# Half-column products in one turn, slice means before W_v W_out, and row factors in all partitions: a change to a graph-attention and slice-attention kernel on one core

## The chip, the core and the metric

One core of a Trainium2 chip runs the whole program. The metric is the device time in microseconds. Every comparison below is made between runs that interleave with the kernel before on the same chip; all runs quoted are in the fast state. The kernel before takes some 2726 us; its runs lie between 2719 and 2735 us, and the sessions' medians between 2724.5 and 2729.7. So I compare ratios within a session where a few us matter.

## The reference

A batch is 512 rows of 256 features; there are 32 batches, each computed alone:

```python
x = x + gnn(layernorm(x), adj, ...)      # two attention layers with residuals
x = x + ffn(layernorm(x), ...)           # slice attention
# gnn: relu(x W1) -> attention without mask (h = x W_fc, e = leaky_relu(f1_i + f2_j))
#      -> elu(elu()) + residual -> relu(. W2) -> attention with mask adj -> residual
# ffn: w = softmax over 64 slices, for 8 heads; tokens = weighted means of fx over rows
#      q, k, v = token W_q, W_k, W_v; att = softmax(q k / 8); out_slice = att v
#      result = (out_slice spread back by w) W_out + b_out
```

All data are float32.

## The kernel before

The kernel does not issue its instructions in program order. It records every operation of all batches with a name of its step ("xnT", "pT" and so on are tiles; "h2", "e", "tokens" are steps), gives each a priority from a table of turns plus the number of its batch times a period, and lets a list scheduler with costs of its own choose, once, at build time, the order on each engine. Each engine then runs its fixed list, waiting on semaphores only. Instructions of three or four batches are thus mixed on every engine. Two more tuples, HEAD and TAIL, shift the priorities of the first and last batches.

```python
TURNS = {"load": -182.4, ..., "h2": -4.8, "e": 4.9, ..., "out": 181.5}
PERIOD, SPARE = 88.0, 0.00
HEAD, TAIL = (-3.1, -0.9, -0.1), (-1.0, -1.3, -1.0)
...
KEPT = 1
...
def start_of(op):                       # in the scheduler
    t = op.ready
    for log in op.logs:                 # the tiles that op uses
        if log not in until:            # not yet allocated
            kept = self.KEPT if log.bufs > self.KEPT and op.age > oldest and log.psum else 0
            if len(slots[log.tag]) <= kept or turn[log.queue][0] is not log:
                return None             # cannot start
```

`op.age` is the batch and `oldest` the oldest unfinished one. So **a batch that is not the oldest may never take the last free PSUM tile of a kind**. There are three kinds, and the rule holds for those with more than one tile:

```python
def mm_tile(shape): return psum.tile(shape, F32, tag="mm", name="mm", bufs=5)
def tr_tile(shape): return psum.tile(shape, F32, tag="tr", name="tr", bufs=2)
def sm_tile(shape): return psum.tile(shape, F32, tag="sm", name="sm", bufs=1)
```

The parts that the change touches are the row factors of the first attention, the logits f2b of the second, the slice tokens with half-column products, and the end of slice attention (shortened):

```python
# factors: exp of 4 numbers a row; two of them are then spread to all partitions
nc.scalar.activation(ex, ex, AF.Exp)
for s in range(2):
    pt = tr_tile([P, N])
    for i in range(NT):
        nc.tensor.transpose(pt[:, ts(i)], ex[:, s, i:i+1].to_broadcast([P, P]), ident)
    nc.scalar.copy(acb[:, s, :], pt)

# h2: logits of the second attention
f2b = new("f2b", [P, N])                                   # SBUF
pt = tr_tile([P, N])
for j in range(NT):
    nc.tensor.transpose(pt[:, ts(j)], h[:, j, D+1:D+2].to_broadcast([P, P]), ident)
nc.scalar.copy(f2b, pt)
# e: for each of four row tiles
nc.vector.scalar_tensor_tensor(e, f2b, h[:, i, D:D+1], mbias[:, i, :], ...)
...
if by_dma("e", b):                      # transposed by DVE blocks and a round trip in DRAM
    flip(e, stage[:, :, ts(i, Q)]); continue
pt = tr_tile([P, NT, P])                # only in the first and the last batch (EDGES):
for j in range(NT):                     # transposed on PE
    nc.tensor.transpose(pt[:, j, :], e[:, ts(j)], ident)

# tokens: 16 products of 64 columns (half of PE's columns) a batch
nc.tensor.matmul(pm[ts(s, C), p, :]..., wfx[:, k, ts(2*p+s, C)], s1T[:, k, :]..., ...)
# vo, gg: tokens times W_v W_out (256 wide), then attention times that (256 wide)
nc.tensor.matmul(pv[:, s, :], tokbd[:, p, :], wvo[:, p, :], start=True, stop=True)
...
nc.tensor.matmul(pg[:, s, :], attT[:, p, :], vo[:, p, :], start=True, stop=True)
```

## Time and profile before

| | before |
|---|---|
| time, median of 3 | 2728.61 us (2726.51 to 2730.74) |
| PE in use | 98% of the span |
| period of a batch in the steady part | 83.1 us |
| all waits of PE | 52 us, of them 13 in 20 steady batches |

The prediction below shows the lines. One thing to know for reading them: a record of PE has a modelled end that overlaps the next record, so neither durations nor their sum tell what an instruction takes from the stream. The distance from start to start does. From those distances I take a nominal pitch for each kind (0.217 us a record of 256 or 257 columns, and so on). The rest of PE's time, labelled waits and unlabelled excess over the pitch together, I call **lost**. This split is used after the result.

### The profile page before, as it was taken

What the parts mean: (1) busy time and instruction counts of PE and PEld (TensorE: products, weight loads), DVE (VectorE), ACT (ScalarE), POOL (GpSimd) and SP (SyncE); (2) the same over time, 40 slices, a digit from 0 to 9 for tenths busy, and PEclk for the clock granted to TensorE, in tenths of its full rate; (3) what the DMA queues carried; (4) which work ended last, traced back from release to release, by engine and by line L of the source; (5) the groups of instructions that cost most, each with busy time, mean ns of one, the idle gap of its engine ahead of it and who ended that gap; (6) DMA issues with size and microseconds to landing.
All of it is one profiled execution on the core that took longest, in us unless ns stands there. A gap on an engine that the chain in (4) does not pass through costs nothing.

```text
span 2725.3 us, 34426 instructions
## 1 busy us (share of the span) xinstructions
PE 2667.5 (98%) x11965; PEld 1988.7 (73%) x11965; DVE 2057.3 (75%) x5126; ACT 1117.4 (41%) x2102; POOL 124.6 (5%) x233
## 2 busy tenths in 40 slices
PE   7999999999999999999999999999999999999997
PEld 5777777777777777777777777777777777777765
DVE  6577777887777877778877778777788777787775
ACT  3443344443444443444434444334444334444332
POOL 1000000000000000000000000000000000000000
PEclk9999999999999999999999999999999999999998
DMA  5226555645555555556454555555565555564521
GB/s 167 58 57 165 135 140 143 168 133 154 139 148 139 148 154 139 138 145 165 133 153 130 158 139 145 157 140 141 147 161 134 158 137 145 140 156 137 133 78 53
DMA packets 465077, 375.35 MB, mean 138 GB/s; under 512 B 86532, under 2 KB 382088, under 8 KB 464904
## 3 DMA queue, kind: packets, MB, share of 16 engines
q1 hardware_dynamic: 461568, 371.01, 51.2%
q10 hardware_dynamic: 3336, 2.14, 0.3%
q8 instruction: 95, 1.56, 0.2%
q14 instruction: 78, 0.64, 0.1%
HBM read 197.96 MB, written 175.11 MB: 137 GB/s over the span
## 4 chain that ended last, share of the span: by engine, by line
PE 73%; DMA 13%; DVE 9%; SPq 2%; issue 2%; ACT 1%; ACTq 0%; POOL 0%; DVEq 0%; POOLq 0%
PE mm L255 70%; DMA o1T<-scr 4%; DMA scr<-s_stage 3%; SPq L255 2%; PE tr L255 2%; DMA s1T<-scr 2%; DVE u L255 1%; DMA w_raw<-scr 1%; DVE u_stage L255 1%; DVE xn L255 1%; DMA scr<-u_stage 1%; DVE xn_stage L255 1%; PE sm L255 1%; DVE vo L255 1%; DVE o1T L255 0%
## 5 line engine op out<-in xcount | busy, mean ns | idle before, releaser
L255 PE MATMUL mm<-wfc,o0T 128*128 128x257 f32 x2048 | 486.1, 379 | 0.0
L255 PEld LDWEIGHTS mm<-wfc,o0T 128*128 128x128 f32 x2048 | 386.2, 189 | 131.1 <-issue 84.9
L255 PE MATMUL mm<-h,pT 128*128 128x257 f32 (+1 forms) x2048 | 467.3, 382 | 0.4 <-ACT u L255 0.2
L255 PEld LDWEIGHTS mm<-h,pT 128*128 128x128 f32 x2048 | 379.9, 189 | 63.1 <-ACT u L255 4.8
L255 DVE TENSOR_TENSOR x<-mm,x 128x512 f32<-128x512 f32 x64 | 44.2, 691 | 292.8 <-PE mm L255 292.8
L255 PE MATMUL mm<-xnT,w 128*128 128x512 f32 x512 | 249.3, 602 | 2.1 <-ACT xnT L255 1.8
L255 PE MATMUL mm<-weff,xn2T 128*128 128x512 f32 x512 | 251.3, 594 | 0.0
L255 PE MATMUL mm<-xn,w 128*128 128x257 f32 x1024 | 244.7, 382 | 4.8 <-DVE w L255 4.8
L255 PE MATMUL mm<-h,p2T 128*128 128x257 f32 x1024 | 242.0, 380 | 0.7 <-ACT p2T L255 0.7
L255 ACT COPY h<-mm 128x257 f32<-128x257 f32 (+1 forms) x384 | 142.2, 370 | 241.2 <-PE mm L255 237.2
L255 PE MATMUL mm<-o1T,w 128*128 128x512 f32 x512 | 227.8, 597 | 10.1 <-DVE o1T L255 9.9
L255 PE MATMUL mm<-gg,wT 128*128 128x256 f32 x1024 | 235.9, 379 | 0.0
L255 PEld LDWEIGHTS mm<-xn,w 128*128 128x128 f32 x1024 | 191.4, 190 | 36.4 <-ACT w L255 5.7
L255 PEld LDWEIGHTS mm<-gg,wT 128*128 128x128 f32 x1024 | 189.6, 190 | 35.1 <-issue 6.5
L255 PEld LDWEIGHTS mm<-h,p2T 128*128 128x128 f32 x1024 | 187.0, 190 | 28.2 <-ACT p2T L255 0.9
L255 PEld LDWEIGHTS mm<-o1T,w 128*128 128x128 f32 x512 | 94.9, 190 | 126.3 <-issue 91.1
L255 DVE STREAM_TRANSPOSE o_stage<-o2T 128x512 f32<-128x512 f32 x64 | 45.6, 712 | 171.0 <-ACT o2T L255 171.0
L255 ACT ACTIVATE e<-e,nmax 128x512 f32<-128x512 f32 x128 | 92.5, 723 | 199.6 <-DVE nmax L255 199.4
L255 ACT ACTIVATE m<-m 128x512 f32<-128x512 f32 x192 | 120.3, 627 | 131.0 <-DVE m L255 130.9
L255 PEld LDWEIGHTS mm<-xnT,w 128*128 128x128 f32 x512 | 92.6, 191 | 68.8 <-issue 50.9
L255 ACT ACTIVATE m<-m,neg 128x512 f32<-128x512 f32 x192 | 138.0, 719 | 3.6
L255 DVE SCALAR_TENSOR_TENSOR u<-m,u 128x512 f32<-128x512 f32 x192 | 131.6, 686 | 9.1 <-ACT m L255 7.7
(144 smaller groups left out, 3917.7 us busy)
## 6 DMA issues: line engine op xcount, KB each, us to landing
scr<-xn_stage SPq DMA_DIRECT2D x240, 128.0 KB, 2.7
scr<-u_stage SPq DMA_DIRECT2D x120, 256.0 KB, 4.3
o1T<-scr SPq DMA_DIRECT2D x30, 1024.0 KB, 6.0
scr<-e_stage SPq DMA_DIRECT2D x120, 256.0 KB, 4.2
p2T<-scr SPq DMA_DIRECT2D x30, 1024.0 KB, 5.4
scr<-w_stage SPq DMA_DIRECT2D x120, 256.0 KB, 4.2
w_raw<-scr SPq DMA_DIRECT2D x30, 1024.0 KB, 6.7
xt<-in_x_dram SPq DMA_DIRECT2D x32, 512.0 KB, 4.6
```

The costliest lines, as they stand in the source:

```text
L255: getattr(getattr(self.nc, op.engine), op.method)(*op.args, **op.kwargs)
```

## The change

The intent: take instructions out of PE's stream, which is the bound. The half-column products are given one priority so that they come in one turn; half as many transposes spread the row factors, by exponentials in all partitions; attention is applied to the 64-wide tokens before they are multiplied by W_v W_out. Two side effects matter later. SBUF is full, so the new tile meanbd takes the room of f2b, which now **stays in the PSUM tile of its transposes**. And turns, period and shifts were chosen anew. The diff is shortened, and some of its lines are put in words:

```diff
-    "load": -182.4, "norm1": -141.0, ... "h2": -4.8, "e": 4.9, ... "out": 181.5,
+    "load": -225.4, "norm1": -221.3, ... "h2": -55.6, "e": -48.0, ... "out": 160.2,
-PERIOD, SPARE = 88.0, 0.00
-HEAD, TAIL = (-3.1, -0.9, -0.1), (-1.0, -1.3, -1.0)
+PERIOD, SPARE = 91.1, 0.00
+HEAD, TAIL = (-0.7, 1.6, 2.6), (0.1, -6.3, 142.4)
...
+            if op.engine == "tensor" and op.half != half:      # scheduler's cost
+                t, half = t + self.SWITCH, op.half             # SWITCH = 0.14
...
+            costs = [0.0 if op.joint else cost for op, cost in zip(ops, costs)]
...  (factors)
-        for s in range(2):
-            pt = tr_tile([P, N]); 4 transposes of ex[:, s]; nc.scalar.copy(acb[:, s, :], pt)
+        pt = tr_tile([P, N]); 4 transposes of sc
+        nc.vector.tensor_scalar(acb[:, 0, :], pt, -beta, 0.0, op0=OP.mult, op1=OP.max)
+        nc.scalar.activation(acb[:, 1, :], pt, AF.Relu, scale=beta)
+        nc.scalar.activation(acb, acb, AF.Exp, scale=-1.0)
...  (h2)
-        f2b = new("f2b", [P, N])
-        pt = tr_tile([P, N])
+        f2b = tr_tile([P, N])
         for j in range(NT):
-            nc.tensor.transpose(pt[:, ts(j)], h[:, j, D + 1 : D + 2].to_broadcast([P, P]), ident)
-        nc.scalar.copy(f2b, pt)
+            nc.tensor.transpose(f2b[:, ts(j)], h[:, j, D + 1 : D + 2].to_broadcast([P, P]), ident)
...  (vo, gg)
-   4 x matmul(pv, tokbd, wvo); DVE adds b_out; attT = copy; 4 x matmul(pg, attT, vo); ACT scales
+   4 transposes of tokbd; tokg = copy; attT = half copies
+   4 x matmul(pa, tokg, attT)  (64 wide); meanbd = half copies
+   4 x matmul(pg, meanbd, wvo) (256 wide); DVE scales and adds b_out
```

## The prediction

> **What bounds the kernel now.** I read the page's busy shares first, then the row of the granted clock, then the list of who waited for whom on PE, and last the order of time on PE, because the first three only say where to look.
>
> ```profile
> PE 2667.5 (98%) x11965; PEld 1988.7 (73%) x11965; DVE 2057.3 (75%) x5126; ACT 1117.4 (41%) x2102; POOL 124.6 (5%) x233
> PEclk9999999999999999999999999999999999999998
> ```
>
> PE is in use for 98% of the span at full clock. The reader should see that nothing else comes near it. But a busy share with modelled ends is not yet a bound, so the waits have to agree:
>
> ```profile
> PE mm L255 <- DMA s1T<-scr: 15.3, 17, 8.5
> PE mm L255 <- DVE o1T L255: 9.9, 16, 1.1
> PE tr L255 <- DVE xn L255: 8.1, 1, 8.1
> PE mm L255 <- DVE w L255: 4.8, 4, 2.3
> ```
>
> The columns are total us, times, longest us. All waits of PE sum to about 52 us of 2725. 8.1 is the start, 8.5 is one wait in the tail, and in the 20 batches between 557.87 and 2219.80 us (the same long piece of the chain recurs at both times) only 13.4 us are waits: 8.1 for o1T, 5.1 for s1T. So a batch takes (2219.80-557.87)/20 = 83.1 us, of which 0.67 is waiting. **The kernel is bound by the issue of TensorE instructions**; a change is worth what it takes out of that stream. The price of an instruction is its distance to the next start, read from the order of time on PE (start, us, what, records):
>
> ```profile
> 1255.32 0.60 PE L255 MATMUL mm<-h,p2T 128*128 128x257 f32 x2
> 1255.75 0.60 PE L255 MATMUL tr<-ident,ex 128*128 128x128 f32 x4
> 1256.19 1.90 PE L255 MATMUL mm<-h,p2T 128*128 128x257 f32 x8
> ...
> 1269.42 3.60 PE L255 MATMUL mm<-h,pT 128*128 128x256 f32 x14
> 1272.94 0.69 PE L255 MATMUL mm<-s1T,wfx 128*64 128x64 f32 x16
> 1273.56 2.00 PE L255 MATMUL mm<-h,pT 128*128 128x256 f32 x8
> 1275.48 0.68 PE L255 MATMUL mm<-s1T,wfx 128*64 128x64 f32 x14
> 1276.09 0.65 PE L255 MATMUL mm<-nrow,bfx 4*64 4x256 f32 x4
> 1276.67 1.13 PE L255 MATMUL mm<-xnT,w 128*128 128x512 f32 x2
> 1277.63 0.59 PE L255 MATMUL mm<-tok,wqk 128*128 128x256 f32 x2
> 1278.07 1.02 PE L255 MATMUL mm<-xnT,w 128*128 128x512 f32 x2
> 1278.92 1.46 PE L255 MATMUL mm<-wvo,tokbd 128*128 128x256 f32 x6
> 1280.22 1.05 PE L255 MATMUL sm<-tok,qbd 128*128 128x64 f32 x8
> 1281.10 0.65 PE L255 MATMUL mm<-wvo,tokbd 128*128 128x256 f32 x2
> ```
>
> A matmul is two records, a transpose one. The row of 4 transposes lasts 1256.19-1255.75 = 0.44, so 0.11 each. 8 records p2T to the next start (1257.93) are 1.74, so 0.217 a record and 0.433 a matmul of 256 or 257 columns. The 64-column product with qbd takes (1281.10-1280.22)/8 = 0.11 a record, 0.22 a matmul. 512 columns cost 0.43 a record. The half-column products (128*64) show the special thing: the 8 records before the second visit take 1.92 where 8 x 0.2165 = 1.73, so **going in costs about 0.19**. Over those 20 batches the records in front of 60 visits exceed their own pitch by 11.74 us, or 0.196 a visit. Coming back: 2, 16 and 14 records last 0.23 (1269.19 to 1269.42), 0.62 and 0.61; with about 0.030 a record and 0.15 for the return, 2 and 16 fit roughly.
>
> **What the Trainium skill says.** "TensorEngine Tiling (Array Packing)", Key Properties: changing the tiling mode drains the array. The trace agrees: about 0.35 us a round trip. "Perfetto Trace Analysis", Identifying the Most-Contended Engine: matmul busy time judges distance to the roofline badly, weight-load share is better. PEld at 73% here would suggest room, yet start-to-start distances leave almost none for this stream; I go by those. "VectorE: DVE Perf Modes", Why PSUM operands drop a tier: any PSUM operand caps fp32 at 1x. That concerns the e step reading f2b from PSUM; its scalar-tensor-tensor already takes 743 ns for 512 columns, which looks like 1x, so I expect no loss. "ScalarE: Activation LUTs", Table sets: relu and copy are in every set; the trace has one table load in all, so the added Relu should bring none.
>
> **The change part by part, on PE.** The order of instructions of the built programs gives the counts.
> 1. Half-column products in one turn. Before: 88 visits to the half-column mode in the program, mostly 3 a batch. After: 36, one a batch in the steady part. 52 fewer x (0.196 + 0.15) = **-18.0 us**. The count of these products is unchanged, 16 + 2 a batch.
> 2. Row factors. Before: 8 transposes of ex a batch; after: 4 of sc. 4 x 0.11 x 32 = **-14 us**. The exponential is now taken of 2 x 512 columns in all partitions: one DVE scalar op from PSUM (as u<-mm or attT, about 0.65), one Relu (0.69) and one Exp of 1024 columns (estimate 1.1, from 0.63 for 512) instead of two 0.585 copies. About 10 us of p2T and xn,w products stand between the transposes and the first h,pT, so it is hidden.
> 3. Mean tokens first. Removed: 4 tokbd products and 4 attT products of 256 columns, 8 x 0.433 = 3.46. Added: 4 transposes of tokbd (0.44), 4 attT,tokg products of 64 columns (0.88), 4 meanbd products of 256 columns (1.73) = 3.05. Attention's 4 transposes stay. So -0.41 x 32 = **-13 us**. The wT product is unchanged.
> 4. Off PE. DVE loses two vo additions (0.67 each), the full attT copy (0.66) and two small ex ops (0.15 each), and gains acb (0.65), two half copies (0.41 each) and four gg ops of 256 columns (about 0.43): +0.9 a batch, 64.3 to 65.2 of 82 us. ACT loses 2 acb copies, f2b (0.59), four gg (0.42 to 0.47), gains Relu, Exp, tokg (0.58) and half copies: about even. Neither sets the end.
>
> Sum on PE: -45 us, 1.4 a batch; the period should go from 83.1 to about 81.7.
>
> **What the waits do.** s1T: before, some 17.2 us of PE work stands between the last xn,w and the first use of s1T, with small waits. After, 11 p2T, 32 h,pT and one small transpose: 43 x 0.434 + 0.11 = 18.8 us. The wait should nearly go: -5 us. o1T: before, from the last h,pT to the o1T product 1275.48 to 1294.86 = 19.4 with a wait of 0.18. After, the fill there is: one turn 2.0, 8 xnT at 0.86 = 6.9, 13 wfc at 0.433 = 5.6, wqk 0.43, qbd 0.88, two sets of transposes 0.88, tokg 0.88, meanbd 1.73: 19.3. Same length, so the same wait, about 0.4 a batch. Tail: in the new order the last batch, after its wh product, has only the products of its own left: about 40 us of PE work. From this trace's durations I lay the chain out: logits and the four e rows 9 to a p2T product at 12, elu and residual 17, norm 21, transposed 23.3, softmax on DVE (12.5 for four tiles) 37.6, sums 40; then the end, which took from 2701.1 to 2725.3 = 24.2 before, plus 1.4 for two more products and copies in series. 66 us, so 26 idle. Before, PE idled about 22 from the same point (15.5 of waits and 4.3 after its last product, the rest slow spots), and the new order also has bare spots ahead (the four h,pT,u transposes, the factors of the last batch). I choose **+8 us** for the tail, the least certain term.
>
> 2728.6 - 45 - 5 + 8 = 2686.6; I say 2685.
>
> **The rivals.**
> (a) A chain of small waits takes the place of the work removed. After qbd's scores, only 4 transposes, one xnT and two wfc (2.17 us) stand before attention's transposes; in the tail, where nothing covered it, that chain took from 2708.53 to 2710.61 = 2.08. Then two wfc (0.87) before tokg, two wfc before meanbd, against some 0.7 to 0.8 for a drain and a half copy. For it: margins of 0.1, DVE 80% used. Against: before, PE had equally short fills and hardly any wait for tok, attT or attbd away from the ends. It would make 0.5 a batch, 16 us: 2701.
> (b) The DMA of o1T gets the bound: the pv products now run without a break, bunching u's transfers with those of s1T. DVE waited 43.7 us for o1T already. At 1 us more a batch: 2715. Against: the fill is as long as before.
> (c) The retuned turns also remove the o1T waits and the tail is no worse: 2728.6 - 45 - 5 - 12 = 2666, over 2% faster. For it: the order was retuned with the mode switch in its model. Against: transfers, the one thing with steady waits, are modelled as before.
>
> **Range and chances.** 2% faster needs 2728.6/1.02 = 2675. The PE sum alone gives 2683; the rest must give 8 more. (c) gets a fifth to a quarter. (a) and (b) both stay within 2%; slower needs 55 us of new waits on top of the 45 saved. Range 2664 to 2708, chances 0.23, 0.76, 0.01.
>
> **What would show it right or wrong.** In the profile after: 36 visits in place of 88, and the records before the one visit of a batch still 0.2 over their pitch (step 1); PE about 45 us less busy (2 and 3); a period of 81.3 to 82.2; PE's waits for s1T below 2 us outside the tail, for o1T near 10, for attbd, attT and meanbd under 0.2 a batch (else rival a); DVE near 2085 us; the last wh product some 66 us before the end. Wrong if o1T or the small copies wait over 0.5 a batch, if 64-column products cost more than 0.22, or if the tail differs by more than 15 us from my +8.

## The result

| | median | range | runs |
|---|---|---|---|
| before | 2729.68 us | 2726.51 to 2733.53 | 4 |
| after | 2729.59 us | 2726.88 to 2732.64 | 4 |

The ratio is 0.9999 (95% interval 0.9981 to 1.0017). A ratio here is the mean time of one kernel's fast runs over that of the other's in the same rounds, so it is not quite the ratio of the medians. The results are correct. Nothing was gained.

The page after: busy shares and the granted clock, in the same form as before.

```profile
PE 2655.7 (97%) x11965; PEld 1970.5 (72%) x11965; DVE 2096.8 (77%) x5190; ACT 1101.5 (40%) x2038; POOL 154.7 (6%) x234
PEclk9999999999999999999999999999999999999988
```

These two lines would send one astray. PE is as busy as before, so it looks as if no work had gone. The one hint is the last two eights of the clock. The order of time on PE in a steady batch, after:

```profile
1258.65 7.09 PE L262 MATMUL mm<-h,pT 128*128 128x257 f32 x32
1265.67 1.15 PE L262 MATMUL mm<-s1T,wfx 128*64 128x64 f32 x32
1266.75 0.65 PE L262 MATMUL mm<-nrow,bfx 4*64 4x256 f32 x4
...
1277.38 1.03 PE L262 MATMUL mm<-wfc,o0T 128*128 128x257 f32 x4
1278.45 1.10 PE L262 MATMUL mm<-attT,tokg 128*128 128x64 f32 x8
1279.39 1.09 PE L262 MATMUL mm<-wfc,o0T 128*128 128x257 f32 x4
1280.46 1.56 PE L262 MATMUL mm<-wvo,meanbd 128*128 128x256 f32 x6
```

The reader is to see that the half-column products stand in one turn, with no wait for s1T before them, and that the steady part went about as planned. In the chain, the same long piece recurs 21 batches later:

```profile
483.09 19.87 PE mm L262 x78
2194.30 19.87 PE mm L262 x78
```

So **the period is 81.5 us, against 83.1 before**. Splitting PE's time at 460 and 2400 us shows where the gain of the steady part went:

| part of the span | nominal pitch, before / after | lost, before / after |
|---|---|---|
| 0 to 460 us (head) | 436 / 421 | 26.8 / 39.2 |
| 460 to 2400 us (steady) | 1906 / 1927 | 31.7 / 14.1 |
| 2400 us to the end (tail) | 288 / 256 | 25.4 / 60.2 |
| sum | 2630 / 2605 | 83.9 / 113.5 |

The first wait, up to PE's first record, counts as lost in the head. The last row of PE's records (11.4 and 12.1 us) has no next start and is left out, so the sums fall short of the spans by that much. PE has 25 us less to do, and loses 18 us less in the steady part. But the head loses 12 us more and **the tail 35 us more**. So the profiled run ends at 2730.5 us, against 2725.3. The tail is where to look. PE's waits after (total us, times, longest us), next to the list that the prediction shows:

```profile
PE tr L262 <- DVE xn L262: 16.6, 2, 8.6
PE tr L262 <- ACT e L262: 7.9, 4, 4.1
PE mm L262 <- DVE o1T L262: 7.5, 13, 1.5
...
PE tr L262 <- DVE u L262: 3.3, 1, 3.3
```

s1T's waits are gone. New are four waits for e and a second one for xn of 8.6 us. There are four waits for e because only an edge batch transposes e on PE. Here are both tails, from the last batch's transposes of h, before and then after:

```profile
2627.48 0.38 PE L255 MATMUL tr<-ident,h 128*128 128x128 f32 x2
2627.70 3.62 PE L255 MATMUL mm<-gg,wT 128*128 128x256 f32 x16
2631.15 1.88 PE L255 MATMUL mm<-weff,xn2T 128*128 128x512 f32 x4
2632.87 0.60 PE L255 MATMUL tr<-ident,e 128*128 128x128 f32 x4
2633.31 1.88 PE L255 MATMUL mm<-weff,xn2T 128*128 128x512 f32 x4
2635.03 0.60 PE L255 MATMUL tr<-ident,e 128*128 128x128 f32 x4
```

```profile
2639.66 7.07 PE L262 MATMUL mm<-gg,wT 128*128 128x256 f32 x32
2646.57 0.60 PE L262 MATMUL mm<-wh,o2T 128*128 128x258 f32 x2
2647.00 0.95 PE L262 MATMUL tr<-ident,h 128*128 128x128 f32 x4
2652.01 1.12 PE L262 MATMUL tr<-ident,e 128*128 128x128 f32 x4 [4.05 <-ACT e L262]
2654.42 1.12 PE L262 MATMUL tr<-ident,e 128*128 128x128 f32 x4 [1.30 <-ACT e L262]
```

Before, the last batch's e rows are transposed between products of its predecessors (gg,wT of one, weff of the other), which fill PE while DVE and ACT work. After, all of the second last batch's 16 wT products (32 records) come first, and then the last batch runs alone for 83.5 us. The stretches from the last wh product to the end, before and after (us, then busy time of PE, PEld, DVE, ACT and POOL with their instructions, granted clock, DMA share and GB/s):

```profile
2626.40:2725.30 98.90, 78.98 (x399) 58.59 (x397) 65.99 (x149) 26.59 (x50) 2.95 (x7) 0.93 0.21 63
```

```profile
2647.00:2730.50 83.50, 53.85 (x236) 38.55 (x234) 41.34 (x94) 18.27 (x33) 2.06 (x4) 0.81 0.03 13
```

No engine is near its limit in the second: a chain is the bound there. But this stretch holds only half of the tail's extra loss. Start-to-start distances, with a pitch of 0.216 us and the last row counted too, give 44 us lost in it, against 27 in its counterpart before, and **25 us lost between 2400 us and this stretch, against 7**: the last batches' earlier steps run nearly bare too, with the wait of 3.3 us for u above and five of 1.2 to 2.5 us for w, x, pT, sc and fm.

The clock falls as well in the last stretch. "TensorE: Matmul & The Clock Gate" of the Trainium skill, in its part on the HAM clock gate, says that the throttle is the default and that idling brings it back. The trace agrees: after the bare stretch of the e rows, the 32 records of p2T take (17.91 - 8.60)/32 = 0.29 us each, against 0.217 in the steady part, with 0.77 of the clock granted. (17.91 us is the distance to the next row, 8.60 the wait before that row.)

### The profile page after: what moved, and what is told of

It is laid out like the page before. It is cut to its first block, busy times and chain, and to the rows that moved or that the text cites. A ratio compares the mean times of both kernels' runs of the same rounds, so it can differ in the third digit from the quotient of the medians.

```text
span 2730.5 us, 34562 instructions
## 1 busy us (share of the span) xinstructions
PE 2655.7 (97%) x11965; PEld 1970.5 (72%) x11965; DVE 2096.8 (77%) x5190; ACT 1101.5 (40%) x2038; POOL 154.7 (6%) x234
## 3 DMA queue, kind: packets, MB, share of 16 engines
q8 instruction: 95, 1.56, 0.2%
## 4 chain that ended last, share of the span: by engine, by line
PE 69%; DVE 17%; DMA 8%; ACT 2%; issue 2%; SPq 1%; POOL 1%; DVEq 0%; ACTq 0%; POOLq 0%
PE mm L262 66%; DMA o1T<-scr 3%; DVE w L262 2%; PE tr L262 2%; DVE u L262 2%; DVE e L262 2%; DMA xt<-in_x_dram 2%; SPq L262 1%; DMA scr<-u_stage 1%; PE sm L262 1%; POOL ln_rstd L262 1%; DVE rs L262 1%; DVE e_stage L262 1%; DVE mx L262 1%; DVE u_stage L262 1%
## 5 line engine op out<-in xcount | busy, mean ns | idle before, releaser
L262 PE MATMUL mm<-wfc,o0T 128*128 128x257 f32 x2048 | 479.5, 380 | 0.0
L262 PE MATMUL mm<-h,pT 128*128 128x256 f32 (+1 forms) x2048 | 459.6, 380 | 2.1 <-DVE pT L262 1.5
L262 PEld LDWEIGHTS mm<-wfc,o0T 128*128 128x128 f32 x2048 | 381.4, 189 | 81.7 <-issue 32.5
L262 PE MATMUL mm<-xn,w 128*128 128x257 f32 x1024 | 264.4, 384 | 8.4 <-DVE w L262 4.3
L262 PE MATMUL mm<-gg,wT 128*128 128x256 f32 x1024 | 249.4, 380 | 0.0
L262 PE MATMUL mm<-weff,xn2T 128*128 128x512 f32 x512 | 232.2, 594 | 0.2 <-ACT xn2T L262 0.2
L262 PEld LDWEIGHTS mm<-h,p2T 128*128 128x128 f32 x1024 | 194.9, 191 | 30.0 <-ACT p2T L262 1.1
L262 ACT ACTIVATE u<-mm,rd 128x256 f32<-128x256 f32 x192 | 90.4, 472 | 263.3 <-DVE rd L262 191.5
L262 DVE SCALAR_TENSOR_TENSOR e<-tr,h,mbias 128x512 f32<-128x512 f32 x128 | 92.4, 743 | 101.9 <-PE tr L262 101.9
L262 PEld LDWEIGHTS mm<-weff,xn2T 128*128 128x128 f32 x512 | 92.8, 191 | 90.3 <-issue 86.9
```

What stands on the lines that cost most here:

```text
L262: getattr(getattr(self.nc, op.engine), op.method)(*op.args, **op.kwargs)
```

## The experiments

Why does the last batch run alone? Two causes suggest themselves, and a third.
- **Theory A, the PSUM tile.** f2b now holds one of the two "tr" tiles from its transposes until the fourth e row. An edge batch needs another "tr" tile for the transposes of e. The scheduler's rule forbids a batch that is not the oldest to take the last free one. So the last batch's e rows cannot begin before the second last batch is finished.
- **Rival B, the shift.** TAIL sets the last batch's priority back by 142.4, so it merely fills gaps and is left over at the end.
- **Rival C, the chain.** The last batch's own path has become longer by two products in series, in a deeper order.

A and B need each other's test, so I ran them as a square of four: f2b of the last batch in PSUM or SBUF, by shift of 142.4 or -1.0.

### x_tail: the shift alone undone

```diff
-HEAD, TAIL = (-0.7, 1.6, 2.6), (0.1, -6.3, 142.4)
+HEAD, TAIL = (-0.7, 1.6, 2.6), (0.1, -6.3, -1.0)
```

> The changed kernel with one number of its order undone: the last batch's priority shift is -1.0 as before, not 142.4. Theory A (the last batch runs alone because f2b now stays in one of the two PSUM tiles for transposes, and a newer batch may not take the last free one while an older is unfinished): no gain, 2720 to 2740 us, and the last batch's transposes of e still start only after the second last batch's wT products. Rival B (it runs alone because the shift puts it last): 2700 to 2712 us. Rival C (its chain is longer because of the two added products and the deeper order): no gain.

Measured: 2733.11 us (6 runs) beside 2724.51 of before; ratio 1.003 (1.0018 to 1.0042). There is no gain, even a small loss. The order of time on PE:

```profile
2645.74 7.09 PE L262 MATMUL mm<-gg,wT 128*128 128x256 f32 x32
2652.67 0.60 PE L262 MATMUL tr<-ident,e 128*128 128x128 f32 x4
2653.95 0.66 PE L262 MATMUL tr<-ident,e 128*128 128x128 f32 x4 [0.68 <-ACT p2T L262]
```

With its priority restored, the last batch's e transposes still come right behind the predecessor's wT products. B alone falls.

### x_f2: f2b of the last batch alone in SBUF

```diff
+        if b == B - 1:
+            held, f2b = f2b, new("f2b", [P, 2, N], tag="acb")[:, 0, :]
+            nc.scalar.copy(f2b, held)
```

A first form with an own tile for f2b did not build: it wanted 208.22 KB a partition of 207.87 free (a later build gave the same message), so with meanbd there is no room for f2b. The last batch no longer needs acb by then, so its room serves.

> The changed kernel, f2b of the last batch alone copied to SBUF as before (in the place of acb, which that batch no longer needs), the shift of 142.4 kept. Theory A: the tile is free but the shift still puts the batch last, so little: 2722 to 2735 us. Rival B: no gain, 2725 to 2735. Rival C: no gain.

Measured: 2727.72 us (20 runs) beside 2724.51; ratio 1.0013 (1.0006 to 1.002). As expected there is almost nothing: the tile is free, but the shift keeps the batch last.

### x_both: both at once

```diff
-HEAD, TAIL = (-0.7, 1.6, 2.6), (0.1, -6.3, 142.4)
+HEAD, TAIL = (-0.7, 1.6, 2.6), (0.1, -6.3, -1.0)
+        if b == B - 1:
+            held, f2b = f2b, new("f2b", [P, 2, N], tag="acb")[:, 0, :]
+            nc.scalar.copy(f2b, held)
```

> Both: f2b of the last batch in SBUF and its shift -1.0. Theory A: the last batch's logits and products overlap the second last batch again; the 17 to 25 us of the tail come back: 2700 to 2712 us, and the end of the last batch's wh products to the end of the span grows with other work in it. Rival B: the same as x_tail. Rival C: 2720 to 2740.

Measured: 2697.29 us (4 runs) beside 2724.51; ratio **0.9897** (0.9879 to 0.9915). The square:

| ratio to before | shift 142.4 | shift -1.0 |
|---|---|---|
| f2b of the last batch in PSUM | 0.9999 (the change) | 1.0030 |
| f2b of the last batch in SBUF | 1.0013 | 0.9897 |

Neither alone helps; together they give back 1.0% of the time, some 28 us. That is a little more than expected (2700 to 2712 us), for the stretch before came back too: from 2400 to 2600 us PE now loses 9 us, where the change lost 25 up to the last stretch. The two added products are in all four corners, so C cannot be the cause of these 28 us. A is right with a supplement: the shift is a sensible answer to a batch that will run alone anyway, and it must go too once the batch can overlap.

### x_b_f2last: the suspected part put into the kernel before

The kernel before with one edit: in the last batch f2b stays in PSUM.

```diff
-        f2b = new("f2b", [P, N])
+        f2b = None if b == B - 1 else new("f2b", [P, N])
         pt = tr_tile([P, N])
         ...
-        nc.scalar.copy(f2b, pt)
+        if f2b is None: f2b = pt
+        else: nc.scalar.copy(f2b, pt)
```

> The kernel before with one thing done: f2b of the last batch alone stays in PSUM. Theory A: the tail of the changed kernel appears here, 2745 to 2760 us, and the transposes of e of the last batch come after the second last batch's wT products. Rivals B and C: the same as before within 5 us, or a little faster for the copy saved.

Measured: 2752.22 us (4 runs) beside 2724.51; ratio **1.0101** (1.0085 to 1.0116). It makes a copy less than the kernel before, and takes 27 us more. In its trace:

```profile
2669.62 7.07 PE L255 MATMUL mm<-gg,wT 128*128 128x256 f32 x32
2676.53 0.60 PE L255 MATMUL tr<-ident,e 128*128 128x128 f32 x4
```

It is the signature of the changed kernel's tail, made by one tile in one batch.

### y_rule: the rule rather than the tile

Is PSUM really short, or is it the scheduler's caution? Here f2b stays in PSUM in every batch, and only the last batch is exempt from the rule (with the shift at -1.0).

```diff
-  kept = self.KEPT if log.bufs > self.KEPT and op.age > oldest and log.psum else 0
+  kept = self.KEPT if log.bufs > self.KEPT and oldest < op.age < 31 and log.psum else 0
```

> The changed kernel with f2b left in PSUM in all batches, but with the last batch exempt from the scheduler's rule that a newer batch may not take the last free PSUM tile of a kind while an older one is unfinished, and with its shift at -1.0. If the rule (not the lack of a tile on the chip, and not the copy) sets the last batch back: as the run with both, 2692 to 2705 us, transposes of e again beside the second last batch's wT products. If the tile itself is short, so that the two batches' transposes wait for one another: 2715 to 2735.

Measured: 2696.27 us (4 runs) beside 2725.93; ratio **0.9900** (0.9882 to 0.9917). The e transposes lie among the predecessor's products again, without a wait:

```profile
2604.11 0.60 PE L262 MATMUL tr<-ident,e 128*128 128x128 f32 x4
2604.54 1.47 PE L262 MATMUL mm<-xn,w 128*128 128x257 f32 x6
2605.84 0.59 PE L262 MATMUL mm<-gg,wT 128*128 128x256 f32 x2
2606.28 0.60 PE L262 MATMUL tr<-ident,e 128*128 128x128 f32 x4
```

y_rule differs from x_tail by this one line of the scheduler, and the ratio goes from 1.0030 to 0.9900. So one "tr" tile suffices for both batches in turn. The reservation alone, presumably meant against a deadlock in the order, kept the last batch back.

### x_b16 and x_a16: half of the batches

Both kernels on the first 16 batches (their outputs are wrong on purpose, since half of them is not written).

```diff
     B, N, D = x.shape
+    B = 16
```

> The kernel before, on the first 16 of the 32 batches only (its output is wrong on purpose: the other half is not written). With the period of 83.1 us read from its trace: 2724.5 - 16 x 83.1 = 1395 us. Together with the next run it splits the time into a slope per batch and the two ends.

> The changed kernel on the first 16 batches only (wrong on purpose in the same way). If the gain per batch is real and the ends take it back (theory A): 2729 - 16 x 81.5 = 1425 us, about 30 us and 2% slower than the kernel before on 16, slope 81.5 against 83.1. If the change gains nothing per batch on the chip: 1400 us or less, the same as before on 16.

Measured: 1400.48 us before, 1422.51 us after, 4 runs each, beside 2727.2 us of before on 32. The changed kernel is 1.6% **slower** on 16 batches and level on 32. With 0.9999 x 2727.2 = 2726.9 for it on 32, the slopes are (2727.2 - 1400.5)/16 = 82.9 and (2726.9 - 1422.5)/16 = 81.5 us a batch. A straight line through these points leaves 1400.5 - 16 x 82.9 = 74 us for the two ends before, and 1422.5 - 16 x 81.5 = 118 us after. This needs no reading of a trace: 1.4 us a batch is gained (the traces say 1.6), and the ends cost 44 us more.

### x_head: the shifts of the first batches alone

```diff
-HEAD, TAIL = (-0.7, 1.6, 2.6), (0.1, -6.3, 142.4)
+HEAD, TAIL = (-2.4, 0.9, 0.6, -0.1), (0.1, -6.3, 142.4)
```

> The changed kernel with the shifts of the first batches alone chosen anew (-2.4, 0.9, 0.6, -0.1 in place of -0.7, 1.6, 2.6). In its trace the first 460 us lose 39 us of PE time against 27 before; with both ends chosen anew 30. If the shifts are the cause of the head's loss: 5 to 9 us less than the changed kernel, 2717 to 2722. If the head's loss comes of what else the new turns do: within 3 us of it.

Measured: 2718.76 us (12 runs) beside 2725.93; ratio 0.9971 (0.9961 to 0.9981). The first 460 us lose 30.9 us, against 39.2 in the changed kernel and 26.8 before. Most of the head's extra loss is thus from how the first batches are placed. What makes up the remaining 4 us was not tested.

### x_joint: the half-column products alone

The kernel before, its order kept, with the 16 products of each batch moved together to the place of the last one (the line that marks these products is left out).

```diff
-        for op in self.order():
+        ops, groups = self.order(), {}
+        for op in ops:
+            if op.half: groups.setdefault(op.age, []).append(op)
+        for op in [x for op in ops if not op.half or op is groups[op.age][-1]
+                   for x in (groups[op.age] if op.half else [op])]:
```

> The kernel before with its order of instructions kept, but the 16 half-column products of a batch moved together to the place of the last of them. Visits to the half-column mode go from 88 to about 32. If a visit costs 0.35 us as read from the trace: 56 x 0.35 = 20 us less, 2700 to 2708 us. If the drains are hidden beside other work: 2720 to 2726.

Measured: 2718.59 us (20 runs) beside 2727.2; ratio 0.9970 (0.9962 to 0.9977). This is a miss: 8.6 us less, not 20. Yet the visits did fall to 32, and their cost went as it should. In the 23 steady batches, the excess of the records in front of a visit, the half-column products and the nrow products together took 60.6 us before and take 41.8 here. Much of the gain was spent at once, it seems because the stream arrives earlier at data that do not come earlier:

```profile
PE mm L263 <- DMA s1T<-scr: 9.2, 1, 9.2
PE mm L263 <- DMA xnT<-scr: 8.9, 12, 1.4
```

Before, PE waited for s1T 17 times and never for the transfer of xnT. Now the former is left once, in the tail, and the latter has 12 waits. The labelled waits between 460 and 2400 us sum to 15.6 us, as before (15.8): they moved. The rest of the shortfall carries no label and was not traced. Here, then, a part of the change alone, in an order tuned for something else, was not worth what it takes out. In the changed kernel, whose turns were chosen with it, the same cost fell to 40.3 us.

### x_ends and y_best: the repaired kernel

x_ends is x_both with the shifts of the first and last four batches chosen anew. y_best is y_rule with such shifts, so its edits to the changed kernel are two lines:

```diff
-HEAD, TAIL = (-0.7, 1.6, 2.6), (0.1, -6.3, 142.4)
+HEAD, TAIL = (-2.2, 0.9, 0.6, -0.1), (0.4, 0.5, -5.1, 1.5)
-  kept = self.KEPT if log.bufs > self.KEPT and op.age > oldest and log.psum else 0
+  kept = self.KEPT if log.bufs > self.KEPT and oldest < op.age < 31 and log.psum else 0
```

> The changed kernel with f2b of the last batch in SBUF, and the priority shifts of the first and last four batches chosen anew. The tail gain of the run with both (2697) stays; the head, which in the changed kernel loses 12 us more than before in its first 460 us, should give back 4 to 8: 2688 to 2694 us. If the head's loss comes of the turns of all batches rather than of the shifts: 2696 or more.

> The candidate to beat both: the last batch exempt from the rule, no copy, both ends' shifts chosen anew. The gains of the two runs above add up if they are separate: 2684 to 2694 us, 1.2 to 1.6% faster than before.

Measured: x_ends 2690.1 us (4 runs) beside 2727.2, ratio 0.9864 (0.9844 to 0.9885); **y_best 2689.97 us** (4 runs) beside 2725.93, ratio **0.9873** (0.9859 to 0.9888). Both are correct and beat both kernels; they cannot be told apart. In y_best the head loses 31.8 us and the tail 31.0. It keeps the 25 us less of nominal work and a steady part with 10.3 us lost.

## Why the prediction was wrong

**The step that failed is the tail term, "+8 us", and behind it a sentence on f2b.** The prediction read in the order of instructions that the last batch would have "only the products of its own left". It took that for a given shape of the new order and priced it. It mentioned f2b in PSUM only for the rate at which DVE reads it, and expected no loss; there it was right, 743 ns a row before and after. It did not ask **how long the tile is held, and who else needs one**. Two tiles, one held through the e step, and a rule on the last free one: that is what set the batch alone, as x_b_f2last and y_rule show. In place of +8 us, the tail's loss grew by 35 us; a tail more than 15 us off was one of the signs of being wrong that the prediction had named. "Trainium Kernel Development and Optimization" of the Trainium skill, Best Practices, says that consistent bubbles can mean that SBUF or PSUM ran out. This case agrees only in part: the bubbles came once, at the end, and PSUM had not run out, for y_rule manages with the same tiles (0.9900). But SBUF was full, so a PSUM tile was kept, so the scheduler's reserve was touched.

**The chain itself was also mis-sized.** It was laid out at 66 us from the last wh product and took 83.5. That is about half of the 35 us. The other half lies before it, where PE loses 25 us against 7: the "bare spots ahead" that the prediction named and left within its +8.

| us from the last wh product | predicted | after |
|---|---|---|
| end of the last p2T product ("a p2T product" in the prediction) | 12 | 23.3 |
| start of xn2's transposes | 21 | 31.9 |
| start of the weff products | 23.3 | 34.1 |
| end of the last xn,w product | 40 | 53.2 |
| end of the span | 66 | 83.5 |

The first row is the largest. I let the p2T products follow each e row. In an edge batch the columns of p2T are interleaved over the four e rows, so the first product needs all four. The code says so, and the order that I had before me has the 16 transposes ahead of all 16 products. After that the 32 records ran at a lower clock (0.77 granted). The last step took 30.3 us instead of 25.6: 0.83 of the clock was granted in it, against 1.00 in the last 24.4 us before, from which it was laid out.

**The head was not priced at all.** It costs 12 us, of which the shifts of the first batches explain 7 to 8 (x_head).

**What was right.** The bound, and the steady part: a period of 81.7 was predicted, 81.5 came. By its terms, per batch in 23 steady batches:

| term | predicted | measured |
|---|---|---|
| fewer transposes, narrower products | -0.84 | -0.85 (nominal pitch; the counts are as in the order) |
| fewer visits to the half-column mode | -0.56 | (40.3 - 60.6)/23 = -0.88 |
| waits of PE that the profile labels | -0.16 | (6.6 - 15.8)/23 = -0.40 |
| rival (a): the small copies | 0 | +0.55 |
| sum | -1.56 | -1.58 |

So the sum was right by luck: visits and waits gave 0.56 us more than predicted, and rival (a) took 0.55. The price of a visit was right, though. Two of the three visits of a steady batch went, and between single records a round trip costs 0.34 us: in the medians before, the last full record takes 0.307 us instead of 0.216, the first two half-column records 0.05 more, the last two 0.10 more, and the first full record after them 0.320. So 0.69 of the 0.88 are visits; the predicted 0.56 is an average over all 32 batches, of 52 visits. The other 0.19 stood as small uneven excess in the rows around them and was not traced. And rival (a) did come, at the size the prediction gave it: around the products of tokg and meanbd PE loses 0.57 us a batch. The prediction had tied it to labelled waits of over 0.2 us a batch, and there are none: look at the steady lines after, where 4 records of wfc last 1278.45 - 1277.38 = 1.07 us instead of 0.87. The wait for the half copy is 0.2 us, and no label shows it: in all 24 steady batches the attT,tokg product starts 0.05 us after the end of ACT's half copy of attT.

Of the other signs that the prediction named: 36 visits, as counted; 0.09 us over the pitch in front of a visit, not 0.2, since half of what it had read as going in was the first record after coming back; s1T's waits gone; o1T's at 7.5 (near 10 was said); DVE at 2096.8 busy (2085). "PE about 45 us less busy" was a bad sign to choose. Busy time fell by 12 us only; slow records in the head and the tail count longer. The time missed the range because of the ends, not of the period: the trace gives 51 us for 32 x 1.6, and the ends took it all.

## What to carry to other kernels

When an operand is left in PSUM to save a copy or room in SBUF, price the time for which its tile is held and look for every other user of that kind of tile, in the edge iterations too, and for rules of allocation that count free tiles. A gain per iteration is only part of the time: read head, steady part and tail apart, or run with half the iterations, which here told slope from ends in two runs. And a shift that a tuner has chosen can be the scar of a blockage; undoing it alone shows nothing until the blockage is gone.

## What the Trainium skill lacked or had wrong

- "TensorEngine Tiling (Array Packing)", Key Properties, has that a change of mode drains the array, but no cost. Here a visit to products of 64 columns and back cost 0.34 us (median of the steady batches before); 0.09 of it shows in front of the visit.
- "Perfetto Trace Analysis", Identifying the Most-Contended Engine, takes the weight-load share, with MFU, in place of matmul busy time as the measure of the distance to the roofline. That does not tell whether PE's stream is full. Here the share stood at 73% with PE's stream full (13 us of labelled waits in 1662 us). After the change it was 72%, while the steady period had fallen by 1.6 us. Neither the weight-load share nor the busy share told the change; start-to-start distances did.
- No page says that a float32 product shows as two records in a profile, or gives their pitch: two records of 0.217 us for 256 or 257 columns, 0.433 us a product, at the full granted clock.
- No page tells that a wait of PE of about 0.2 us can go unlabelled in a profile: 0.57 us a batch around two small copies here, found only by comparing pitches.
